# A causal attention stage without TensorE transposes: turns by VectorE and DMA, x loaded a batch sooner, work between the pairs spread evenly

## The chip, the core and the metric

The kernel runs on one NeuronCore of one Trainium2 chip. The core has a matrix engine (TensorE, PE in the profile; its weight loads are PEld), VectorE (DVE), ScalarE (ACT), GpSimd (POOL) and SyncE (SP), whose queue issues almost all DMAs here. Each engine works through its own list in order; semaphores tie the lists together. Matmuls write to PSUM, which has eight banks of 128 x 512 float32. The metric is device time in microseconds (us) from one launch to its end; less is better.

## What is computed

Two attention models run one after the other on the same `x`. The change touches the first, causal attention with a layer norm ahead and a residual; the second (two layers of windowed attention with a gated feed-forward part) is left as it is.

```python
x = x + _L0_attn_ref(_layernorm(x, axis=-1), wq, bq, wk, bk, wv, bv, wo, bo)
x = x + _L0_ffn_ref(_layernorm(x, axis=-1), ...)

def _L0_attn_ref(x, wq, bq, wk, bk, wv, bv, wo, bo):      # x: 4 batches, 1024 tokens, 256 wide
    q = proj(wq, bq); k = proj(wk, bk); v = proj(wv, bv)  # 16 heads of 16
    scores = jnp.einsum('bhqd,bhkd->bhqk', q, k) * scale
    mask = jnp.triu(jnp.full((t, t), NEG, jnp.float32), k=1)
    attn = jax.nn.softmax(scores + mask, axis=-1)
    out = jnp.einsum('bhqk,bhkd->bhqd', attn, v)
    return out.transpose(0, 2, 1, 3).reshape(b, t, d) @ wo + bo
```

Everything is float32.

## The kernel before

**Tiling.** A *chunk* n is four heads of one batch: 4 batches x 4 = 16 chunks, b, c = divmod(n, 4). Its four heads lie in four 32-row strips of two buffers `qbuf` and `kbuf` (head j in rows 32j to 32j+15; row 32j+16 of `kbuf` is a constant). So four small matmuls, one per strip, run in TensorE side by side. Each score is computed twice: first as `s`, queries on partitions, from which VectorE takes each query's maximum (line 375 with the mask on the diagonal, line 380 elsewhere), then as `t`, keys on partitions and the maximum already subtracted, of which ScalarE takes the exponential into `et` (line 388). GpSimd zeroes the masked part of the diagonal blocks (line 394). The product of `et` with `v_sb` accumulates in `av`; a column of ones in `v_sb` gives the softmax's denominator in row 16 of each strip.

**Order.** The list of each engine is written out by hand (`manual_schedule`). A chunk has twelve *units*. In unit u, `pair(n, u, 0)` issues two `t` of chunk n and two `s` of chunk n+1, `products(n, u-2)` follows, then `pair(n, u, 1)` with the other two heads, then the unit's *fillers*. Units have 512, 384, 256, 128, five times 512, 384, 256 and 128 columns. Before chunk 0 there is a round n = -1 with maxima alone; chunk 15 has no `s`.

**Fillers** are set out by `fillers(n)`:
- `norm`, `prep_x`, `prep_a`, `prep_b`, in the second chunk of a batch, for the next batch: statistics and `xn` on VectorE, the transpose `pxn` on TensorE, its copy to `xnT` on ScalarE, then `v`, with the bias added by VectorE;
- `project`: a quarter of q or k (`pp`), copied with its bias to `dense` by ScalarE; `spread`: eight DMAs on SP from `dense` to the strips of `qbuf` and `kbuf`;
- `put_maxima`: four transposes `pm` of the maxima, which VectorE subtracts from `qbuf` into `qTm` (line 413), the operand of `t`;
- `put_out`: four transposes `po` of the copied `av`, then division by the denominator into `y_sb`;
- `out_a`, `out_b`, `out_c`: transposes `pot`, output projection `pr`, residual and next layer norm; after the last one of a batch x goes to DRAM (`x_keep`) and, where there is one, x of batch b+2 is loaded.

**PSUM.** `t` has three banks (`pat`), `s` three (`pas`), and `av` and all fillers share two (`pa1`).

The second stage turns its operands with VectorE transposes of 32 x 32 blocks into `turned` (lines 783 to 806), from which sixteen DMAs (line 814) carry the blocks to their places in `ring_sb`. It starts with the matmuls `pq`, `pk`, `pv` of line 715.

Of the kernel before, what the change touches and what calls it, by code (L numbers as in the profile page):

```python
# [49 lines left out]
def kernel_body(  # L50
# [26 lines left out]

    la = ctx.enter_context(tc.tile_pool(name="la", bufs=1))
    actx = ExitStack()
    xpool = actx.enter_context(tc.tile_pool(name="xpool", bufs=2))  # L80
# [86 lines left out]

    with actx:
# [3 lines left out]
        a3 = actx.enter_context(tc.tile_pool(name="a3", bufs=3))  # L172
# [3 lines left out]
        pas = actx.enter_context(tc.tile_pool(name="pas", bufs=3, space=PSUM))  # L176
        pa1 = actx.enter_context(tc.tile_pool(name="pa1", bufs=2, space=PSUM))

        def one(name):
            return pa1.tile([P, 512], F32, tag="one", name=name)  # L180
# [23 lines left out]
        qbuf = [aw.tile([P, T], F32, name=f"qbuf{i}") for i in range(3)]  # L204
        kbuf = [aw.tile([P, T], F32, name=f"kbuf{i}") for i in range(4)]

        nmax = []
        for i in range(NW):
            m = aw.tile([P, 4, STRIP], F32, name=f"nmax{i}")
            nmax.append(m)  # L210

        def clear():

            nc.gpsimd.memset(qbuf[1], 0.0)
            nc.gpsimd.memset(kbuf[1], 1.0)
            for v in v_sb:
                nc.gpsimd.memset(v[:, :, H * VW :], 0.0)
                nc.gpsimd.memset(
                    v[:, :, 0 : H * VW].rearrange("p k (h s) -> p k h s", s=VW)[
                        :, :, :, ONE : ONE + 1  # L220
                    ],
                    1.0,
                )
            nc.gpsimd.memset(qbuf[2], 0.0)
            for i in (2, 3):
                nc.gpsimd.memset(kbuf[i], 1.0)
# [10 lines left out]
        stats, xnTs, qTms, dense, avs_, mxs = {}, {}, {}, {}, {}, {}  # L237
        qTs, kTs = (lambda n: qbuf[n % 3]), (lambda n: kbuf[n % 4])

        def norm(b, t0=0, t1=NW):  # L240

            if t0 == 0:
                xnTs[b] = a1.tile([P, 2, T], F32, tag="xnT", name=f"xnT_{b}")
# [9 lines left out]
        def prep_x(b, t2):  # L253

            for t in (2 * t2, 2 * t2 + 1):
                xn = a3.tile([P, D], F32, tag="xn", name=f"xn_{b}_{t}")
                mean, rs = stats.pop((b, "t", t))
                nc.vector.tensor_scalar(xn, xs[b][:, t, :], mean, rs, ALU.subtract, ALU.mult)
                stats[b, "xn", t] = xn

        def prep_a(b, t2):

            pt = one(f"pxn_{b}_{t2}")
            for i in range(2):
                xn = stats.pop((b, "xn", 2 * t2 + i))
                for c in range(2):
                    o = c * 256 + i * P
                    nc.tensor.transpose(pt[:, o : o + P], xn[:, c * P : (c + 1) * P], ident)
            nc.scalar.copy(
                xnTs[b][:, :, t2 * 256 : (t2 + 1) * 256], pt.rearrange("p (c n) -> p c n", c=2)  # L270
            )

        def prep_b(b, t2):

            pv = one(f"pv_{b}_{t2}")
            for i in range(2):
                t = 2 * t2 + i
                for c in range(2):
                    nc.tensor.matmul(  # L279
                        pv[:, i * D : (i + 1) * D], lhsT=xnTs[b][:, c, t * P : (t + 1) * P],  # L280
                        rhs=wv_sb[:, c, :], start=(c == 0), stop=(c == 1),
                    )
            for i in range(2):
                nc.vector.tensor_tensor(
# [4 lines left out]
                    rows_c[:, 0, :].rearrange("p (h d) -> p h d", h=H),  # L289
                    ALU.add,  # L290
# [4 lines left out]
            )  # L295

        def project(b, d, which, h):
# [8 lines left out]
            for k in range(2):  # L306
                nc.tensor.matmul(  # L307
                    pp[:, 0:256], lhsT=wt[:, k, d * P : (d + 1) * P], rhs=xnTs[b][:, k, ts],
                    start=(k == 0), stop=(k == 1),
# [18 lines left out]
        def pair(n, u, pr):  # L328
# [15 lines left out]
            if th:  # L344
# [3 lines left out]
                for j, h in enumerate(th):  # L348
                    r = slice(32 * h, 32 * h + 32)
                    todo.append((j, 0, ts[h][:, c0:512], kTs(n)[r, kt * P : (kt + 1) * P],  # L350
                                 qTms[n][r, qb * 512 + c0 : (qb + 1) * 512]))
            if sh:
# [6 lines left out]
                for j, h in enumerate(sh):  # L359
                    r = slice(32 * h, 32 * h + 32)  # L360
# [4 lines left out]
            if sh:  # L365
                if i >= 4 and piece == 0 and pr == 0:
                    mxs[n + 1, i] = a5.tile([P, 4, 2], F32, tag="mx", name=f"mx_{n + 1}_{i}")
                for h in sh:
                    if i >= 4:
                        acc = mxs[n + 1, i][:, h, piece : piece + 1]  # L370
                    else:
                        acc = nmax[i][:, h, ONE : ONE + 1]
                    if diag:
# [3 lines left out]
                            scale=1.0, scalar=-3.0e38, op0=ALU.add, op1=ALU.max, accum_out=acc,  # L377
# [3 lines left out]
                if piece and (pr or first):  # L381
                    nc.vector.tensor_reduce(
                        nmax[i][:, :, ONE], mxs.pop((n + 1, i)), AX.X, ALU.max
                    )
# [17 lines left out]
        def put_maxima(n, qb):  # L402

            if qb == 0:
                qTms[n] = a2.tile([P, T], F32, tag="qTm", name=f"qTm_{n}")
            pm = one(f"pm_{n}_{qb}")
            for i in range(4):
                nc.tensor.transpose(
                    pm[:, i * P : (i + 1) * P],
                    nmax[4 * qb + i].rearrange("p j s -> p (j s)"), ident,  # L410
                )
            qs = slice(qb * 512, (qb + 1) * 512)
            nc.vector.tensor_tensor(qTms[n][:, qs], qTs(n)[:, qs], pm, ALU.subtract)

        def products(n, u):
# [3 lines left out]
            if kt == 0:  # L419
                avs_[n, "acc"] = one(f"av_{n}_{qb}")  # L420
            av = avs_[n, "acc"]
            ets, c0 = avs_.pop((n, u))
            for j in range(4):
                nc.tensor.matmul(  # L424
                    av[32 * j : 32 * j + 32, c0:512],
                    lhsT=v_sb[b % 2][:, kt, VW * (4 * c + j) : VW * (4 * c + j) + STRIP],
                    rhs=ets[j // 2][:, j % 2, c0:512],
                    start=(kt == 0), stop=(kt == 4 * qb + 3),
                )
            if kt == 4 * qb + 3:  # L430
                avs = a2.tile([P, 512], F32, tag="avs", name=f"avs_{n}_{qb}")
# [3 lines left out]
        def put_out(n, qb):  # L435

            b, c = divmod(n, NC4)
            avs = avs_.pop((n, "out", qb))
            po = one(f"po_{n}_{qb}")
            for i in range(4):  # L440
# [833 lines left out]
```

## Time and profile before

| what | value (us where no unit is given) |
|---|---|
| median of 3 runs (lowest, highest) | 1977.33 (1976.79, 1978.14) |
| profiled execution, its own time | 1976.66 |
| its span | 1974.9 |
| first pair of chunk 0 | 54.2 |
| first pair of chunk 15 | 716.7 |
| first matmul of the second stage (`pq`) | 760.0 |
| chunks 4, 5, 6, 7 (a whole batch) | 45.8, 46.7, 42.4, 44.8 |
| chunk 13 (no next batch to prepare) | 39.5 |
| causal stage, share of SP's DMAs in 54 to 717 us | 9% of the DMA engines |
| granted TensorE clock, whole span | 0.988 of full speed |

The chunk times are the distances between the first pairs of successive chunks on TensorE's timeline. In the stretch from 54 to 717 us VectorE is busy for 476.6 of 663 us, ScalarE for 365.5 and GpSimd for 135.6.

How the profile is read: in a list of groups each line has the source line, the engine, the operation, what it writes and reads, its shape and count, then the busy time in us and the mean of one in ns, then the engine's idle time just ahead and what ended it. A float32 matmul shows as two instructions (two passes). In a timeline the columns are the start, the duration, the engine, the line and operation; in brackets the idle time before it and what ended it.

### The profile page before, as it was taken

The page shows a single profiled execution, that of the slowest core. Times are in us where ns is not written, and L with a number is a line of the kernel's source. Part 1 is how long each engine was busy: PE and PEld are TensorE (multiplying, and loading weights), DVE is VectorE, ACT ScalarE, POOL GpSimd, SP SyncE. Part 2 cuts the span into 40 slices and gives each one's busy share as a digit, 9 for nine tenths or more (in the row PEclk, how much of TensorE's full clock was granted, in tenths as well). Part 3 has the DMA queues.
Part 4 walks back from the last instruction along what each step waited for, and adds up shares of the span by engine and source line. Part 5 has one row for each costly group of instructions (what it writes and reads, how often), then busy time and mean ns, then how long its engine had stood idle before and what let it go on. Part 6 is the DMA issues. An engine that isn't in the chain of part 4 may idle for free.

```text
span 1974.9 us, 46934 instructions
## 1 busy us (share of the span) xinstructions
PE 1921.1 (97%) x17356; PEld 1091.1 (55%) x17356; DVE 1364.2 (69%) x4196; ACT 1000.8 (51%) x2627; POOL 932.4 (47%) x1177
## 2 busy tenths in 40 slices
PE   8999999999999997989899999999999999999999
PEld 5444444444444434646565666666666666566575
DVE  6686777677667745676776776776777687677633
ACT  1556555555555563545455555555545544555521
POOL 3122122112211115775765765765675676676521
PEclk8999999999999999999899999999999999999999
DMA  3021010101001001045555555565566565665520
GB/s 96 19 72 23 12 54 3 26 28 33 15 20 33 1 1 68 10 83 91 101 87 95 97 106 90 107 125 102 92 145 113 99 115 106 108 113 99 102 49 22
DMA packets 763347, 136.26 MB, mean 69 GB/s; under 512 B 733952, under 2 KB 756208, under 8 KB 762608
## 3 DMA queue, kind: packets, MB, share of 16 engines
q1 hardware_dynamic: 762864, 133.00, 34.6%
q8 instruction: 138, 2.26, 0.5%
q14 instruction: 89, 0.73, 0.1%
q10 hardware_dynamic: 256, 0.26, 0.1%
HBM read 20.99 MB, written 8.39 MB: 15 GB/s over the span
## 4 chain that ended last, share of the span: by engine, by line
PE 86%; DVE 5%; SPq 3%; issue 1%; POOL 1%; DMA 1%; ACT 1%; DVEq 0%; ACTq 0%; POOLq 0%
PE t L364 15%; PE pag L1074 14%; PE av L424 7%; PE pf L1098 7%; PE pw L984 5%; PE pq L715 5%; PE pk L715 5%; PE plo L942 4%; PE pv L715 4%; PE ls L862 3%; PE pp L307 3%; SPq L814 3%; PE s L364 3%; PE pr L472 1%; PE pv L279 1%
## 5 line engine op out<-in xcount | busy, mean ns | idle before, releaser
L388 ACT ACTIVATE et<-t 128x512 f32<-128x512 f32 (+2 forms) x744 | 327.6, 492 | 278.1 <-PE s L364 248.5
L364 PE MATMUL s<-kbuf,qbuf 32*128 32x512 f32 (+3 forms) x1440 | 381.7, 532 | 2.2 <-DVE nmax L375 1.5
L364 PE MATMUL t<-qTm,kbuf 32*128 32x512 f32 (+2 forms) x1488 | 371.2, 532 | 0.8 <-ACT et L388 0.2
L394 POOL TENSOR_SCALAR_AFFINE_SELECT et<-et 128x256 f32<-128x256 f32 x256 | 103.8, 407 | 462.0 <-ACT et L388 461.8
L1074 PE MATMUL pag<-hnT,w 128*128 128x512 f32 x704 | 312.0, 593 | 0.8 <-DVE hnT L1058 0.8
L375 DVE CUSTOM_DVE_ANT_0 junk<-s,mask_c 128x512 f32<-128x512 f32 (+1 forms) x480 | 216.4, 488 | 89.6 <-PE s L364 85.8
L895 ACT ACTIVATE e<-e,lnmx 128x192 f32<-128x192 f32 (+2 forms) x512 | 224.1, 439 | 47.4 <-DVE lnmx L888 46.9
L364 PEld LDWEIGHTS t<-qTm,kbuf 32*128 32x128 f32 x1488 | 135.5, 183 | 169.4 <-ACT et L388 127.7
L909 POOL TENSOR_SCALAR e<-e,lrsum 128x192 f32<-128x192 f32 (+2 forms) x512 | 205.7, 423 | 19.5 <-DVE lrsum L906 13.9
L1074 PEld LDWEIGHTS pag<-hnT,w 128*128 128x128 f32 x704 | 131.7, 190 | 142.5 <-issue 134.2
L380 DVE TENSOR_REDUCE mx<-s 128x1 f32<-128x512 f32 x240 | 154.7, 686 | 68.1 <-PE s L364 66.3
L754 POOL TENSOR_TENSOR rn<-ss,mhalf 128x16 f32<-128x16 f32 x64 | 188.1, 2939 | 5.3
L1098 PE MATMUL pf<-w,act 128*128 128x256 f32 x768 | 173.1, 379 | 0.0
L751 POOL TENSOR_TENSOR rot<-rot,m 128x1024 f32<-128x1024 f32 x64 | 151.1, 2362 | 38.6 <-DVE m L732 34.9
L424 PE MATMUL av<-et,v_sb 128*32 128x512 f32 (+3 forms) x1536 | 163.5, 498 | 0.6 <-POOL et L394 0.6
L1098 PEld LDWEIGHTS pf<-w,act 128*128 128x128 f32 x768 | 146.1, 190 | 26.4 <-issue 7.2
L1088 DVE SCALAR_TENSOR_TENSOR act<-pag,cols_sb,ge 128x512 f32<-128x512 f32 x80 | 59.3, 741 | 141.6 <-ACT ge L1087 102.9
L364 PEld LDWEIGHTS s<-kbuf,qbuf 32*128 32x128 f32 x1440 | 140.4, 183 | 17.5 <-DVE nmax L375 6.0
L888 DVE CUSTOM_DVE_ANT_0 e<-ls,mask_h 128x192 f32<-128x192 f32 x408 | 116.8, 350 | 22.2 <-PE ls L862 22.1
L984 PE MATMUL pw<-wlo,loT 128*128 128x256 f32 x512 | 127.5, 393 | 0.7 <-ACT loT L975 0.7
L715 PE MATMUL pq<-wqkv,hT 128*128 128x512 f32 x256 | 122.6, 602 | 3.8 <-ACT hT L697 3.8
L756 POOL TENSOR_TENSOR rot<-rot,rn 128x1024 f32<-128x1024 f32 x64 | 121.7, 1901 | 5.0
(287 smaller groups left out, 3214.3 us busy)
## 6 DMA issues: line engine op xcount, KB each, us to landing
ring_sb<-turned SPq DMA_DIRECT2D x896, 96.0 KB
qbuf<-dense SPq DMA_DIRECT2D x128, 32.0 KB
x_keep<-x SPq DMA_DIRECT2D x4, 1024.0 KB
xr<-x_keep SPq DMA_DIRECT2D x8, 512.0 KB
out_dram<-y_sb SPq DMA_DIRECT2D x16, 256.0 KB
kbuf<-dense SPq DMA_DIRECT2D x120, 32.0 KB
x<-in_x_dram SPq DMA_DIRECT2D x3, 1024.0 KB
wqkv<-in_wqkv_dram SPq DMA_DIRECT2D x2, 1536.0 KB
```

Of the source, the lines that this page charges most:

```text
L364: nc.tensor.matmul(o, lhsT=lhsT, rhs=rhs, start=True, stop=True)
L375: nc.vector.tensor_tensor_reduce(out=junk[:, 0:w], in0=ss[h][:, 0:w], in1=mask_c[:, 512 - w : 512], scale=1.0, scalar=-3.0e38, op0=ALU.add ...
L380: nc.vector.tensor_reduce(acc, ss[h][:, 0:w], AX.X, ALU.max)
L388: nc.scalar.activation(et[:, h % 2, c0:512], ts[h][:, c0:512], AF.Exp, scale=ASCALE)
L424: nc.tensor.matmul(av[32 * j : 32 * j + 32, c0:512], lhsT=v_sb[b % 2][:, kt, VW * (4 * c + j) : VW * (4 * c + j) + STRIP], rhs=ets[j // 2] ...
L715: nc.tensor.matmul(pq[i], lhsT=lhs[c], rhs=wt[:, c, i * INNER : (i + 1) * INNER], start=(c == 0), stop=(c == 1),)
L754: nc.gpsimd.tensor_tensor(rn[:, :, 0], ss, mhalf, ALU.pow)
L895: nc.scalar.activation(e[:, i, lo:nk], e[:, i, lo:nk], AF.Exp, bias=nmx[:, h : h + 1], scale=-1.0, accum_out=sums[:, h : h + 1],)
L909: nc.gpsimd.tensor_scalar(e[:, i, lo:nk], e[:, i, lo:nk], rsum[:, h : h + 1], 1.0, ALU.mult, ALU.mult)
L984: nc.tensor.matmul(pw[:, 0:D], lhsT=oT[:, c, :], rhs=wt[:, c, :], start=(c == 0), stop=(c == 3))
L1074: nc.tensor.matmul(pg[half], lhsT=wt[:, c, ff * P : (ff + 1) * P], rhs=hnT[:, c, :], start=(c == 0), stop=(c == 1),)
L1098: nc.tensor.matmul(pf[:, 0:D], lhsT=act[:, f, i * P : (i + 1) * P], rhs=wt[:, f, :], start=(f == 0), stop=(f == NF - 1),)
```

## The change

- Maxima: VectorE writes them into one tile `nmax`, in 16 columns for each half of the queries; `put_maxima` transposes it on VectorE (`mt`), writes it by four DMAs to a DRAM tile `way`, and reads it back by one into row 16 of each strip of `qbuf`. Row 16 of `kbuf` is -1, so `t` itself subtracts the maximum; `qTm` is gone. `s` uses only the 16 rows of q and k.
- Output: `put_out` transposes `avs` on VectorE (32 x 32 blocks), GpSimd divides, `put_oT` transposes back and four DMAs carry the strips to `oT`, the operand of `out_b`. `out_a` is gone.
- Input: for batches 1 to 3 `xn` is made by GpSimd, turned by VectorE into `xturn` and carried to `xnT` by sixteen DMAs for each half of a batch (`turn_x`). It starts in the first chunk of a batch and goes on in the second.
- The bias of v goes through `wo` once (`bias`) into the row that is added to x.
- `project`, `prep_b` and `out_b` issue each matmul as four of 32 columns (`strips`).
- ScalarE copies `v` and the output projection; GpSimd adds the residual and makes `y_sb`.
- In units without a matmul filler, `products` is issued in two halves, one after each pair.
- `s` and the fillers share four banks, `av` has one, `t` keeps three. `qbuf` has four buffers, x three; x of batch 2 is loaded in chunk 1, x of batch 3 after batch 0 is done.
- Memsets at the start: three of q and k go to VectorE ahead of the first norm, three of later buffers to GpSimd in the round n = -1.

```diff
-    xpool = actx.enter_context(tc.tile_pool(name="xpool", bufs=2))
+    xpool = actx.enter_context(tc.tile_pool(name="xpool", bufs=3))
...
-        pas = actx.enter_context(tc.tile_pool(name="pas", bufs=3, space=PSUM))
-        pa1 = actx.enter_context(tc.tile_pool(name="pa1", bufs=2, space=PSUM))
+        pas = actx.enter_context(tc.tile_pool(name="pas", bufs=4, space=PSUM))
+        pa1 = actx.enter_context(tc.tile_pool(name="pa1", bufs=1, space=PSUM))
         def one(name):
-            return pa1.tile([P, 512], F32, tag="one", name=name)
+            return pas.tile([P, 512], F32, tag="s", name=name)
...
+        xturn = aw.tile([P, GRP, 2, 4, 32], F32, name="xturn")
+        oT = aw.tile([P, 2, T], F32, name="oT")
         def clear():
-            nc.gpsimd.memset(qbuf[1], 0.0)
-            nc.gpsimd.memset(kbuf[1], 1.0)
+            nc.vector.memset(qbuf[1], 0.0)
+            nc.vector.memset(kbuf[1], -1.0)
+            nc.vector.memset(qbuf[2], 0.0)
...
+        def clear_more():
+            nc.gpsimd.memset(kbuf[2], -1.0)
+            nc.gpsimd.memset(qbuf[3], 0.0)
+            nc.gpsimd.memset(kbuf[3], -1.0)
...
+        def strips(o, lhsT, rhs, k):
+            for r in range(0, P, STRIP):
+                nc.tensor.matmul(
+                    o[r : r + STRIP], lhsT=lhsT[:, r : r + STRIP], rhs=rhs,
+                    start=(k == 0), stop=(k == 1), skip_group_check=True,
+                )
...
+        def turn_x(b, g, i):
+            for t in (2 * i, 2 * i + 1):
+                nc.vector.transpose(
+                    xturn[:, t].rearrange("p c j r -> p (c j r)"), stats.pop((b, "xn", GRP * g + t))
+                )
+            if i == 0:
+                return
+            dst = xnTs[b][:, GRP * g : GRP * g + GRP].rearrange("p t c n -> p (t c) n")
+            src = xturn.rearrange("p t c j r -> p (t c) j r")
+            for d in range(4):
+                for a in range(4):
+                    j = (a + d) % 4
+                    nc.sync.dma_start(
+                        dst[32 * j : 32 * j + 32, :, 32 * a : 32 * a + 32],
+                        src[32 * a : 32 * a + 32, :, j, :],
+                    )
...
         def put_maxima(n, qb):
-            pm = one(f"pm_{n}_{qb}")
-            for i in range(4):
-                nc.tensor.transpose(
-                    pm[:, i * P : (i + 1) * P],
-                    nmax[4 * qb + i].rearrange("p j s -> p (j s)"), ident,
-                )
-            qs = slice(qb * 512, (qb + 1) * 512)
-            nc.vector.tensor_tensor(qTms[n][:, qs], qTs(n)[:, qs], pm, ALU.subtract)
+            mt = a2.tile([P, STRIP], F32, tag="mt", name=f"mt_{n}_{qb}")
+            nc.vector.transpose(mt, nmax[:, qb, :])
+            way = keep4.tile([4 * GRP, P], F32, tag="way", name=f"way_{n}_{qb}")
+            for a in range(4):
+                nc.sync.dma_start(
+                    way[:, 32 * a : 32 * a + 32], mt[32 * a : 32 * a + 4 * GRP, :]
+                )
+            nc.sync.dma_start(
+                qTs(n)[ONE:P:STRIP, qb * 512 : (qb + 1) * 512],
+                way.rearrange("(j i) x -> j (i x)", j=4),
+            )
...
         def put_out(n, qb):
+            t1 = a1.tile([P, 16, 32], F32, tag="t1", name=f"t1_{n}_{qb}")
+            nc.vector.transpose(t1.rearrange("p q s -> p (q s)"), avs_.pop((n, "out", qb)))
+            rec = a2.tile([P, 16, 1], F32, tag="rec", name=f"rec_{n}_{qb}")
+            nc.vector.reciprocal(rec, t1[:, :, ONE : ONE + 1])
+            nc.gpsimd.tensor_tensor(
+                t1[:, :, 0:HD], t1[:, :, 0:HD], rec.to_broadcast([P, 16, HD]), ALU.mult
+            )
+            avs_[n, "t1", qb] = t1
+        def put_oT(n, qb):
             b, c = divmod(n, NC4)
+            t3 = a1.tile([P, 512], F32, tag="t3", name=f"t3_{n}_{qb}")
+            nc.vector.transpose(t3, avs_.pop((n, "t1", qb)).rearrange("p q s -> p (q s)"))
+            for j in range(4):
+                r = (c % 2) * 64 + j * HD
+                nc.sync.dma_start(
+                    oT[r : r + HD, c // 2, qb * 512 : (qb + 1) * 512],
+                    t3[STRIP * j : STRIP * j + HD, :],
+                )
...
+            if c == 0:
+                if b:
+                    quarters(n, b, 1, 3, 0, 2, 4, 6, 8)
+                    outs(n, 7, b - 1, 2)
+                    outs(n, NU, b - 1, 3)
...
+                put(n, 9, spread, n + 2, 1)
+                put(n, NU, spread, n + 3, 1)
+            if c == 0 and more:
+                for i, u in enumerate((5, 7, 9, 10)):
+                    put(n, u, norm, b + 1, 2 * i, 2 * i + 2)
+                put(n, 8, prep_x, b + 1, 0)
+                put(n, 10, turn_x, b + 1, 0, 0)
+                put(n, 10, prep_x, b + 1, 1)
+                n += 1
+                put(n, 0, turn_x, b + 1, 0, 1)
+                put(n, 1, prep_x, b + 1, 2)
+                put(n, 2, prep_x, b + 1, 3)
+                put(n, 3, turn_x, b + 1, 1, 0)
+                put(n, 4, turn_x, b + 1, 1, 1)
+                quarters(n, b + 1, 0, 0, 5, 6, 8, 10)
+                n += 1
+                quarters(n, b + 1, 0, 4, 0, 2, 3, 4)
...
                 for u in range(NU):
                     pair(n, u, 0)
                     m, w = (n, u - LAG) if u >= LAG else (n - 1, u - LAG + NU)
+                    apart = 0 <= n < NCH - 1 and not any(fn in on_pe for fn, _ in f[u])
+                    apart = apart and UNITS_T[w][1] > 0
                     if m >= 0:
-                        products(m, w)
-                    if n % NC4 == 1 and u == 8:
-                        put_maxima(n + 1, 0)
+                        products(m, w, 0 if apart else None)
                     pair(n, u, 1)
+                    if m >= 0 and apart:
+                        products(m, w, 1)
                     for fn, a in f[u]:
                         fn(*a)
```

A slot NU in `put` is unit 0 of the next chunk. In the new lists SP has, from unit 11 of a batch's first chunk on: the five DMAs of `put_maxima(n + 1, 1)`, in chunk 1 the loads of `wqkv`, the tables and `wlo`, the eight DMAs of `spread(n + 3, 1)`, the sixteen of `turn_x(., 0, 1)`, in chunk 5 and 9 the store `x_keep` (in 5 the load of x too), the four of `put_oT(n - 1, 1)`, and the sixteen of `turn_x(., 1, 1)`.

## The prediction

> **What bounds the kernel now.** I read the busy rows first, then the groups of the first 800 us by form, then TensorE's timeline block by block. The change lies in the causal stage, which ends with the first matmul `pq` at 760.0 us.
>
> ```profile
> PE 1921.1 (97%) x17356; PEld 1091.1 (55%) x17356; DVE 1364.2 (69%) x4196; ACT 1000.8 (51%) x2627; POOL 932.4 (47%) x1177
> L364 PEld LDWEIGHTS t<-qTm,kbuf 32*128 32x128 f32 x1488 | 135.5, 183 | 169.4 <-ACT et L388 127.7
> ```
>
> TensorE is busy for 97% of the span, so one would think that every removed matmul pays. But the weight loads of `t` stood 127.7 us behind `et`: the next `t` waits until ScalarE has emptied a bank. The timeline shows one such wait:
>
> ```profile
> 342.64 0.59 PE L364 MATMUL s<-kbuf,qbuf 32*128 32x512 f32 x1
> ...
> 343.16 0.43 PE L424 MATMUL av<-et,v_sb 128*32 128x128 f32 x8
> 343.29 1.29 DVE L380 TENSOR_REDUCE mx<-s 128x1 f32<-128x512 f32 x2 [1.13 <-PE s L364]
> 343.31 1.08 ACT L388 ACTIVATE et<-t 128x512 f32<-128x512 f32 x2 [0.64 <-PE s L364]
> 343.51 0.69 PE L364 MATMUL t<-qTm,kbuf 32*128 32x512 f32 x1
> 343.52 0.69 PE L364 MATMUL s<-kbuf,qbuf 32*128 32x512 f32 x1
> 343.95 0.69 PE L364 MATMUL t<-qTm,kbuf 32*128 32x512 f32 x1
> 344.04 0.69 PE L364 MATMUL s<-kbuf,qbuf 32*128 32x512 f32 x1
> ```
>
> The second `t` starts 0.44 us after the first, when the first exponential has ended; the second `s` 0.09 later, when the first maximum has freed the third `s` bank.
>
> From start to start, a block of TensorE takes for 512/384/256/128 columns: a pair 1.07/0.86/0.64/0.43, products 1.00/0.78/0.57/0.36, a projection 1.06, `pv` or `pr` 1.925, four transposes 0.585. These values repeat to 0.01. A pair is longer only when too little lies ahead of it: 1.36 after a block of 0.57, 1.57 after 0.36, 2.04 right after a pair (which then takes 0.96), 1.07 after 1.00 or more. In each case the pair ahead, the block between and the excess make **1.93 us** (1.07+0.57+0.29; 1.07+0.36+0.50): a floor under the step from pair to pair (1.60, 1.25, 0.97 for the other widths). Chunks 0 to 14 (54.2 to 716.7) take 662.5 us: blocks 602.8, plus 49.9 for the floor, plus 9.8 unexplained.
>
> **The change, part by part.**
>
> *Transposes.* `pm`, `po`, `pot` and three batches of `pxn` go: 32+32+16+12 = 92 blocks of 0.585, 54 us of TensorE. But most stood between pairs that the floor keeps apart: a unit of 512 columns with a transpose takes 4.00 us (1.07+1.00+1.07+0.585+0.27), and one without filler takes 4.00 too (2.04+1.00+0.96, chunk 13).
>
> *Products in halves.* Where a unit has no filler, half a product block stands ahead of each pair: two floors, 3.86, each half costing a further 0.15 (the products' time beyond their columns).
>
> *Four `s` banks.* The second `s` no longer waits for VectorE; what is left is ScalarE. The 0.09 of the timeline makes the floor 1.85 (I take 1.53, 1.18, 0.92).
>
> *Strips.* A projection in four 32-column strips costs what products with 2x512 columns cost, as those too are four strips with 128 rows: 1.00, `pv` and `pr` 1.85. Bounds: that, and 0.4 more each if the sixteen loads show.
>
> Adding the new order of blocks by these prices: blocks 557.9, floors 57.9, **615.8 us** for chunks 0 to 14, against 652.7 before by the same sum. So 54 us of transposes are worth 37.
>
> *VectorE, ScalarE, GpSimd.* Out go `qTm` 32x0.683, `y_sb` from `po` 13.6, the `v` addition 13.4, `nmax` 10.5, and `x`, `xn`, `y_sb` of 14, 24 and 30 instructions, 90 us in all; in come 64 transposes of 128x512 at 0.67 and 24 of 128x256 at 0.40 (the rows of `turned`), with the small `mt` some 58 us. A chunk has about 29 us of maxima on VectorE, so the first chunk of a batch, which now has the whole norm (four times 1.35: two `st` of 0.41, two `mv` of 0.18, one `ve` of 0.17), gets 41 us against TensorE's 40. Units 9 to 11 there give it 9.7 us (maxima 6.2, two norms, a turn of 0.8) for TensorE's 7.2: it ends 2.8 us behind, and the next pair waits about 1.3. Three times: +4. ScalarE gains 4 us and GpSimd 65, both far from full.
>
> *The turn through SP.* A batch's `xn` is turned by VectorE into `xturn`, one buffer for four tiles, and sixteen DMAs carry it to `xnT`. `turn_x(.,1,0)`, unit 3 of a batch's second chunk, writes `xturn` again, so VectorE, in order, waits there until all sixteen have read it. The second stage has this very scheme, and its wait:
>
> ```profile
> 866.45 2.03 SPq L814 DMA_DIRECT2D ring_sb<-turned  x3
> ...
> 870.34 1.25 DVE L783 STREAM_TRANSPOSE turned<-rot 128x1024 f32<-128x1024 f32 x1 [4.76 <-DMA ring_sb<-turned]
> ```
>
> VectorE goes on 1.9 us after the last issue ended. Issues of the same shape (8x32) stand 0.65 apart. SP's queue from the chunk's start: the maxima `mt` at +3.0 (VectorE's lag); four `way` DMAs 2.4, their landing 2.0, the read 0.6 (+8.0); spread of chunk n+3, 8x0.63 (+13.0); sixteen turns, 10.4 (+23.4); VectorE free at +25.3. It reached the wait near +14.5. Behind it stand t3 of the last chunk, the four maxima of unit 4 and then the turn of tiles 6 and 7. TensorE fills its four `s` banks in unit 4 and is out at 12.4 (units 0 to 3 by the prices above) + 1.3 + 3.7 (unit 4) = +17.4; a bank is free at 25.3+0.8+0.65+0.1 = 26.9. **9.5 us** idle.
>
> The Trainium skill speaks against such DMAs: "DMA: Bandwidth & Descriptors", Anatomy of one DMA, puts about 2.0 us of fixed cost on each (for GpSimd's path). Sixteen in a row would be 32 us, an estimate; the rows show them overlapped, 10.4+1.9, and I take the rows.
>
> An idle TensorE also loses its clock. By the rows:
>
> ```profile
> 760.03 3.79 PE L715 MATMUL pq<-wqkv,hT 128*128 128x512 f32 x4 [3.09 <-ACT hT L697]
> 763.61 3.14 PE L715 MATMUL pk<-wqkv,hT 128*128 128x512 f32 x4
> 766.59 1.88 PE L715 MATMUL pv<-wqkv,hT 128*128 128x512 f32 x4
> ```
>
> The same four matmuls take 3.79, 3.14, then 1.88 after 3.09 us idle: 3.2 lost. The skill ("TensorE: Matmul & The Clock Gate", Part 1) says that an idle window of some 3.4 us halves the clock until a busy one has passed, which would lose 1.7, an estimate. I take 3.0. So 12.5 for the batches at chunks 5 and 9. In chunk 1 the loads of `wqkv`, tables and `wlo` come into SP's queue just before the spread; in this trace those 3.1 MB fill the DMA engines for 11 us (103 to 114), where the spread's reuse of semaphores makes SP wait for them: +7.5, and TensorE comes 1.1 earlier (no `out_b` in unit 0): 21. Together **46**, less 2 of floors that lie in it. Bounds: 20 (SP ahead by half) and 60.
>
> *Other moves on queues.* The maxima of the upper half pass SP with five DMAs, 7 us, ahead of a use four units (13 us) on: hidden, unless SP is behind; after the turns it is, but that chunk's end is then later too. In chunk 5 SP also waits 3.5 us (its wait for `x_keep<-x` here: 7.0 in 2) before the load of x for batch 3; that falls behind the first turn and delays the second, whose columns are first used in the next chunk: hidden by some 10 us. Otherwise the earlier load of x brings nothing: no row of before waits for x after the start.
>
> *Start.* Here
>
> ```profile
> 14.07 6.84 DVE L258 TENSOR_SCALAR xn<-x,mv,rs_a 128x256 f32<-128x256 f32 x4 [1.13 <-POOL rs_a L158]
> ```
>
> four `xn` take 6.84 us beside GpSimd's memsets (13.98 to 19.5), 0.41 each elsewhere. Those memsets move: three to VectorE at its idle start, three later. That gives 5 us, of which ScalarE's DMA issues (to 18.0) keep half. The first chunk of maxima, bound by VectorE, loses 2 us of work. Together -4; between -6 and 0, if VectorE's three memsets meet GpSimd's (1.7 each, as here).
>
> *End.* Chunk 15 loses 3 us of transposes; after it the chain `avs`, two VectorE transposes, four DMAs takes 7.9 us where 4.75 were, at a colder clock: +1 net, between -2 and +4.
>
> **Sum.** 615.8 + 4 + 46 - 2 + 5 (half of the unexplained 9.8, as four banks absorb some) = 668.8 for chunks 0 to 14: +6.3. With -4 and +1: +3.3. The profiled run took 1976.66 (span 1974.9), so 1980.0; the median of the runs is 0.67 above it: **1981 us**, no change within 0.2% (4 us, which is about what a measurement here can tell).
>
> **Rivals.**
> 1. *The turn is mostly hidden.* The same, with SP ahead: VectorE's lag doesn't hold `way`, loads overlap the spread. The wait is 20 instead of 46: 1955. For it: SP is mostly free in this stage; its longest waits there are for `dense` (318.5 us in 23). Against: the 4.76 wait above. From 38 on it isn't faster. Chance 0.27.
> 2. *The floor stays.* ScalarE alone sets 1.93, and four banks and halves buy nothing: floors 72.7 instead of 57.9, +15: 1996. For it: the stall is the same for diagonal maxima, which VectorE takes 0.08 longer for. It decides as soon as the floor is over 1.87. Chance 0.23.
> 3. *Strips don't overlap* in sequence: 0.35 more on each block, +28: 2008. Against: the products' 1.00. Chance 0.05.
>
> The forecast (1970 to 1990) has 0.45. Range 1953 to 2003, which leaves out the lower third of rival 1 and the third. Faster by over 4 us (under 1973.4): rival 1 and 0.05 of the middle, 0.32. Within: 0.20 of the middle. Slower (over 1981.3): the middle's other 0.20, rivals 2 and 3: 0.48.
>
> **What would show it.** Right: no transposes but four `pxn` on TensorE before 760 us; VectorE waits of about 10, 10 and 18 us for `xnT<-xturn` in chunks 1, 5, 9, TensorE's clock low after each; 512-unit without filler about 3.7. Wrong: waits under 5 us; units of 3.3 (no floor) or 4.0; `pp` blocks of more than 1.1; the second stage changed by more than 2 us.

## The result, and the profile after

| | before | changed |
|---|---|---|
| median of 8 runs (lowest, highest) | 1977.74 (1971.23, 1983.43) | 1986.57 (1981.74, 1991.55) |
| ratio, 95% interval | | 1.0037 [1.0020, 1.0053] |
| profiled execution, its own time / its span | 1976.66 / 1974.9 | 1991.55 / 1989.8 |
| first pair of chunk 0 | 54.2 | 59.1 |
| chunks 0 to 14 | 662.5 | 663.8 |
| chunks 1, 5, 9 | 46.7, 46.7, 46.7 | 65.2, 52.9, 57.1 |
| chunks 2, 3, 4, 13, 14 | 42.4, 44.8, 45.8, 39.5, 39.0 | 42.3, 42.9, 40.6, 37.0, 35.4 |
| first pair of chunk 15 to the first `pq` | 43.3 | 43.7 |
| first `pq` to the last matmul | 1211.3 | 1219.6 |

All times in us. The change made the kernel slower by 0.4%. The profiled execution of the changed kernel was the slowest of its eight, so the difference of the two profiles, 14.9 us, is 6 us above that of the medians.

The page of the changed kernel: busy time by engine, the granted clock in 40 slices of 50 us, and the weight loads of `t` that the prediction started from.

```profile
PE 1899.3 (95%) x19234; PEld 1033.1 (52%) x19234; DVE 1350.0 (68%) x4092; ACT 1005.3 (51%) x2646; POOL 1029.5 (52%) x1268
...
PEclk7959998998899998989999999999999999999999
...
L415 PEld LDWEIGHTS t<-qbuf,kbuf 32*128 32x128 f32 x1488 | 145.4, 190 | 171.4 <-ACT et L439 114.8
```

TensorE's busy time fell by 22 us and the time rose. The wait of these loads for `et` fell only from 127.7 to 114.8 us. The row of the clock is the new thing: a 5 in the third slice, where before no slice was under 8. Of the twelve chunks other than 1, 5 and 9, nine are 1.6 to 6.3 us shorter, and 2, 6 and 10 are as long as before. Chunks 1, 5 and 9 took that back, and they are those in which most of `turn_x` works.

The wait that was forecast is there. VectorE's timeline in chunk 1, then SP's:

```profile
116.37 0.08 DVE L427 DVE_READ_ACCUMULATOR2_ANT nmax<- 128x1 f32 x1
130.68 0.77 DVE L295 STREAM_TRANSPOSE xturn<-xn 128x256 f32<-128x256 f32 x2 [14.23 <-DMA xnT<-xturn]
131.38 0.67 DVE L507 STREAM_TRANSPOSE t<-t 128x512 f32<-128x512 f32 x1
```

```profile
118.09 0.51 SPq L374 DMA_DIRECT2D kbuf<-dense  x1
118.70 10.47 SPq L305 DMA_DIRECT2D xnT<-xturn  x16
```

VectorE stands 14.2 us until the sixteen DMAs have read `xturn`. They are issued in 10.5 us, and the last read ends 1.5 us after. In chunk 5 the wait is 8.2 us, in chunk 9 6.8. TensorE runs out of `s` banks behind it and stands for 8.5, 6.0 and 4.6 us; in chunk 1:

```profile
132.68 1.21 PE L415 MATMUL s<-kbuf,qbuf 16*128 16x512 f32 x1 [8.52 <-DVE mx L433]
```

The half clock wasn't expected in that measure. Busy time in windows of 10 us (PE, PEld, DVE, ACT, POOL, each with its count), then the granted clock, the DMA engines' share and GB/s:

```profile
20.00:30.00 10.00, 6.75 (x66) 3.20 (x58) 4.53 (x16) 1.79 (x4) 0.00 (x0) 0.82 0.20 44
30.00:40.00 10.00, 9.57 (x54) 4.82 (x58) 7.93 (x26) 0.00 (x0) 4.93 (x4) 0.50 0.39 108
40.00:50.00 10.00, 10.00 (x64) 3.48 (x56) 4.87 (x8) 0.65 (x2) 0.00 (x0) 0.50 0.12 38
...
110.00:120.00 10.00, 9.90 (x68) 4.25 (x72) 3.16 (x18) 3.17 (x10) 6.53 (x9) 0.50 0.69 204
...
140.00:150.00 10.00, 10.00 (x58) 2.28 (x58) 3.90 (x7) 3.50 (x8) 0.62 (x1) 0.54 0.22 35
```

Two of the same windows in the kernel before:

```profile
30.00:40.00 10.00, 10.00 (x40) 6.15 (x41) 9.04 (x31) 0.00 (x0) 0.00 (x0) 0.61 0.30 66
140.00:150.00 10.00, 10.00 (x84) 5.00 (x84) 6.77 (x30) 4.49 (x13) 3.52 (x7) 1.00 0.00 0
```

In the changed kernel TensorE is busy all the time from 40 to 50 us and from 140 to 150, and the clock is half for all or nearly all of it. The rule that the prediction weighed, that a busy window brings the clock back, does not fit this. Nor did the wait start the half clock of chunk 1: by the clock's records it lasts from 101.4 to 149.2 us, so it begins 15 us before VectorE stands and some 23 us before TensorE does.

### The profile page after: what moved, and what is told of

The parts are those of the page before. It is cut to its first block, busy times and chain, and to the rows that moved or that the text cites. A ratio compares the mean times of both kernels' runs of the same rounds, so it can differ in the third digit from the quotient of the medians.

```text
span 1989.8 us, 51315 instructions
## 1 busy us (share of the span) xinstructions
PE 1899.3 (95%) x19234; PEld 1033.1 (52%) x19234; DVE 1350.0 (68%) x4092; ACT 1005.3 (51%) x2646; POOL 1029.5 (52%) x1268
## 4 chain that ended last, share of the span: by engine, by line
PE 85%; SPq 5%; DVE 4%; issue 2%; DMA 2%; POOL 1%; ACT 1%; ACTq 0%; DVEq 0%; POOLq 0%
PE t L415 15%; PE pag L1144 14%; PE pf L1168 8%; PE av L478 7%; PE pw L1054 6%; PE pq L785 5%; PE pk L785 5%; PE pv L785 5%; PE plo L1012 4%; PE ls L932 4%; SPq L884 3%; PE pp L252 3%; PE pv L252 2%; PE s L415 2%; PE pr L252 1%
## 5 line engine op out<-in xcount | busy, mean ns | idle before, releaser
L415 PE MATMUL s<-kbuf,qbuf 16*128 16x512 f32 (+3 forms) x1440 | 387.8, 561 | 19.5 <-DVE mx L433 19.1
L415 PE MATMUL t<-qbuf,kbuf 32*128 32x512 f32 (+2 forms) x1488 | 402.5, 559 | 2.5 <-ACT et L439 2.4
L415 PEld LDWEIGHTS t<-qbuf,kbuf 32*128 32x128 f32 x1488 | 145.4, 190 | 171.4 <-ACT et L439 114.8
L979 POOL TENSOR_SCALAR e<-e,lrsum 128x192 f32<-128x192 f32 (+2 forms) x512 | 205.7, 423 | 20.4 <-DVE lrsum L976 14.9
L478 PE MATMUL av<-et,v_sb 128*32 128x256 f32 (+5 forms) x2240 | 187.9, 408 | 4.3 <-POOL et L445 2.8
L1168 PEld LDWEIGHTS pf<-w,act 128*128 128x128 f32 x768 | 145.8, 190 | 26.6 <-issue 7.2
L415 PEld LDWEIGHTS s<-kbuf,qbuf 16*128 16x128 f32 x1440 | 143.6, 191 | 29.7 <-DVE mx L433 23.5
L427 DVE CUSTOM_DVE_ANT_0 junk<-s,mask_c 128x512 f32<-128x512 f32 (+3 forms) x240 | 106.9, 485 | 61.6 <-PE s L415 59.1
L427 DVE CUSTOM_DVE_ANT_0 junk<-s,mask_c,mx 128x512 f32<-128x512 f32 (+3 forms) x240 | 121.0, 546 | 37.6 <-PE s L415 36.4
L958 DVE CUSTOM_DVE_ANT_0 e<-ls,mask_h 128x192 f32<-128x192 f32 x408 | 116.9, 350 | 23.2 <-PE ls L932 23.2
L478 PEld LDWEIGHTS av<-et,v_sb 128*32 128x32 f32 x2240 | 45.3, 109 | 163.6 <-issue 119.0
```

What stands on the lines that cost most here:

```text
L415: nc.tensor.matmul(o, lhsT=lhsT, rhs=rhs, start=True, stop=True)
L427: nc.vector.tensor_tensor_reduce(out=junk[:, 0:w], in0=ss[h][:, 0:w], in1=mask_c[:, 512 - w : 512], scale=1.0, scalar=mxs[n + 1, i][:, h : ...
L478: nc.tensor.matmul(av[32 * j : 32 * j + 32, lo:hi], lhsT=v_sb[b % 2][:, kt, VW * (4 * c + j) : VW * (4 * c + j) + STRIP], rhs=ets[j // 2][ ...
L979: nc.gpsimd.tensor_scalar(e[:, i, lo:nk], e[:, i, lo:nk], rsum[:, h : h + 1], 1.0, ALU.mult, ALU.mult)
L1168: nc.tensor.matmul(pf[:, 0:D], lhsT=act[:, f, i * P : (i + 1) * P], rhs=wt[:, f, :], start=(f == 0), stop=(f == NF - 1),)
```

## The experiments

Three theories were put against each other.

1. *The turn.* The loss is the wait for `xturn`: what lies ahead of the sixteen DMAs in SP's queue sets it.
2. *The array's work.* The clock comes back only when enough of the array works in a window, and `s` with 16 rows instead of 32 does half the work in the same time.
3. *Code.* TensorE's additional matmuls shift where its code is loaded, and the second stage stalls there.

Under the second theory one number can be worked out from the trace for each window of 3.41 us (all low stretches, but for the one that the end of a run cuts off, are multiples of it): the sum over the matmuls of rows x columns of the array in use, times the columns streamed, as a share of what a 128 x 128 array does when it streams 512 columns in 0.43 us (`pq`: four such passes in 1.71 us). It is called the **share** below.

### Two buffers for the turn

```diff
-        xturn = aw.tile([P, GRP, 2, 4, 32], F32, name="xturn")
+        xturns = [aw.tile([P, GRP, 2, 4, 32], F32, name=f"xturn{g}") for g in range(2)]
...
         def turn_x(b, g, i):
+            xturn = xturns[g]
```

> Two xturn buffers, one for each half of a batch, so that VectorE's turn of tiles 4 and 5 no longer waits for the first sixteen DMAs. Theory 1 (the wait for xturn is the loss): chunks 1, 5 and 9, now 65.2, 52.9 and 57.1 us, come to about 40 each, the 14.2, 8.2 and 6.8 us of VectorE waiting go, and the time falls by 45 to 55 us to 1930 to 1942. If in addition the clock stays low for as long as the array does little (theory 2), chunk 1 stays at half clock for some 20 us from its start, as a low window lies ahead of the wait, and it takes 47 rather than 40. Rival (SP's queue is the bound, and the wait only turns up at the next use, of xnT or of mt): less than 15 us gained.

Measured: 1974.78, ratio to before 0.9978 [0.9966, 0.9989], some 12 us less than the changed kernel. Expected were 45 to 55. In the profile, which is of its slowest execution, chunks 1, 5 and 9 took 58.0, 51.7 and 57.3: the first gained 7.2 us, the others 1.2 and nothing. VectorE no longer waits for `xturn`. TensorE does, at the first projection of the new batch in unit 5 (its timeline):

```profile
127.38 1.06 PE L416 MATMUL s<-kbuf,qbuf 16*128 16x512 f32 x1
131.84 1.51 PE L252 MATMUL pp<-xnT,wq_sb 128*32 128x256 f32 x12 [3.41 <-DMA xnT<-xturn]
```

The rival was right: the same sixteen DMAs have a second waiter, the reader of `xnT`, and the gain stayed under its 15 us. The clock stayed low from 102 for 41.0 us in chunk 1, and for 27.3 us in chunk 9.

### The turn ahead of the spread

```diff
-                put(n, NU, spread, n + 3, 1)
+                put(n, NU + 2, spread, n + 3, 1)
```

> spread(n+3, 1), eight DMAs, is issued two units later, behind the first sixteen turn DMAs instead of ahead of them; one xturn buffer as in the changed kernel. Theory 1 (VectorE waits for the last turn DMA, and what lies ahead in SP's queue sets that): the wait of chunk 1 falls from 14.2 to about 4 us, those of chunks 5 and 9 from 8.2 and 6.8 to about 3 and 2, the total by 18 to 28 us to 1959 to 1969. Rival (the DMAs' own transfer, not the queue, or the loads of 3.1 MB in chunk 1, set it): less than 8 us gained.

Measured: 1973.81, ratio 0.9975 [0.9965, 0.9984], some 12 us less than the changed kernel. VectorE's waits fell from 14.2, 8.2 and 6.8 to 8.2, 4.4 and 2.7, chunks 1, 5 and 9 to 55.6, 49.7 and 50.1. So the order in SP's queue sets the wait, as theory 1 says, but in chunk 1 only by 6 instead of 10 us: the sixteen issues, which now stand right behind the 3.1 MB of loads, took 15.1 instead of 10.5 us, 1.8 of them in waits for loads `wlo` and `tab`. The gain of the time was two thirds of the lower end expected.

### s over 32 rows

```diff
-                    r = slice(32 * h, 32 * h + HD)
+                    r = slice(32 * h, 32 * h + STRIP)
```

> s reads 32 rows of each strip again instead of 16; all else as in the changed kernel. Row 16 then takes part: it holds an older chunk's maximum times -1, a shift of all scores of a query, which the softmax takes out again. Theory 2 (the clock comes back only when a 3.4 us window has enough rows x columns of the array at work, about 0.38 of the whole, and pairs at half clock with 16 rows give 0.29 to 0.38 where 32 rows would give 0.37 to 0.45): the low stretch at the start shrinks from 23.9 to about 10 us, those after the waits in chunks 1 and 9 end some 10 us sooner each; first pair of chunk 0 at about 52 instead of 59.1, total 12 to 17 us less, 1970 to 1975. Rival (the clock looks at idle time alone): no change, 1984 to 1989, low stretches of 24, 48 and 20 us as before.

Measured: 1982.53, ratio 1.0021 [1.0013, 1.0029], some 3 us less than the changed kernel, a quarter of what was expected. The low stretches did what theory 2 says: 10.2 us instead of 23.9 at the start, 23.9 instead of 47.8 in chunk 1, 13.7 instead of 20.5 in chunk 9; first pair of chunk 0 at 54.3. The same windows as above:

```profile
30.00:40.00 10.00, 9.57 (x66) 4.96 (x65) 7.60 (x26) 0.00 (x0) 4.93 (x4) 0.61 0.33 81
40.00:50.00 10.00, 9.49 (x116) 4.05 (x112) 8.46 (x18) 1.94 (x6) 0.00 (x0) 1.00 0.20 68
...
140.00:150.00 10.00, 10.00 (x100) 3.13 (x96) 8.40 (x20) 6.39 (x13) 1.78 (x4) 1.00 0.35 103
```

The time gained less than the clock, because the wait for the turn ends when SP is done and TensorE is only sooner at it: it stood 17.4, 7.8 and 8.1 us in chunks 1, 5 and 9, where it stood 8.5, 6.0 and 4.6. Chunks 1 and 9 gained 3.4 and 3.2 us in this profile, the start 4.8.

### The kernel before, with s over 16 rows

The same line of the kernel before, the other way round: `32 * h + 32` becomes `32 * h + HD` for `s`.

> The kernel before, with s cut to the 16 rows of q and k, as in the changed kernel; nothing else. Theory 2 (array work in a window decides when the clock comes back): the two low stretches at the start, 6.8 and 10.2 us, grow to 20 us or more together with s alone at work there, first pair of chunk 0 at 57 to 60 instead of 54.2; chunks 0 to 14 as before, as nothing makes TensorE idle there. Total 2 to 5 us more. Rival (idle time alone): no change, low stretches 6.8 and 10.2.

Measured: 1989.28, ratio 1.0054 [1.0037, 1.0071], 10.7 us more, twice the most expected. First pair of chunk 0 at 57.0, with a stretch of 17.1 us instead of 10.2. The expectation was wrong in that nothing would happen in the chunks: chunks 1, 5 and 9 took 48.2 instead of 46.7, chunk 4 49.0 instead of 45.8. Its windows, the kernel before first:

```profile
255.00:260.00 5.00, 5.00 (x35) 2.33 (x35) 3.87 (x7) 2.75 (x5) 0.00 (x0) 1.00 0.00 0
260.00:265.00 5.00, 5.00 (x30) 1.78 (x29) 4.24 (x10) 2.17 (x4) 0.70 (x1) 1.00 0.51 210
```

```profile
255.00:260.00 5.00, 5.00 (x30) 2.07 (x28) 4.48 (x11) 2.56 (x5) 0.69 (x1) 0.92 0.00 0
260.00:265.00 5.00, 5.00 (x22) 1.24 (x24) 1.90 (x4) 1.67 (x3) 0.00 (x0) 0.50 0.00 0
```

Nobody waits here. TensorE is busy for all of the ten us in both, and in the second the clock falls to half: the window from 255.8 us has a share of 0.37. The rows alone cost half a per cent, with no wait on a turn in the program.

### The bias of v ahead of ScalarE's issues

```diff
-            nc.scalar.copy(bv[:, 0:D], pb[:, 0:D])
-            po = one("pbias_o")
+            nc.scalar.copy(bv[:, 0:D], pb[:, 0:D])
+            stats["bv"] = bv
+
+        def bias():
+            bv = stats.pop("bv")
+            po = one("pbias_o")
...
-        plan[n][0] += [(spread, (0, 1, nc.scalar)), (spread, (1, 0)), (spread, (1, 1))]
+        plan[n][0] += [(bias_a, ()), (spread, (0, 1, nc.scalar)), (spread, (1, 0)), (spread, (1, 1))]
```

The lines ahead of `def bias` become `bias_a`; `bv` gets a tile of its own.

> The bias of v is transposed and copied at the end of unit 0's projections, ahead of ScalarE's four DMA issues, and only its product with wo stays in unit 1, so TensorE doesn't stand 3.25 us. Theory A (this stall and the half clock that follows put the start back): first pair of chunk 0 at 51 to 55 instead of 59.1, total 4 to 8 us less. Rival B (round -1 is bound by VectorE's maxima and falls to half clock with or without the stall): under 2.5 us gained, first pair at 57 or later.

Measured: first pair of chunk 0 at 51.7, 7.4 us sooner, as theory A says; low stretches at the start of 6.8 and 3.4 us. The time was 1984.07, ratio 1.0027 [1.0014, 1.0040]: 2 us less, which the intervals don't separate from nothing. In this profile chunks 5 and 9 differ from the changed kernel's by +3.8 and -3.7 us though no edit is there: a low stretch begins where the windows of 3.41 us happen to lie. That is what the runs of these kernels scatter by. The stall itself, on the changed kernel's timeline:

```profile
23.83 3.57 ACTq L374 DMA_DIRECT2D kbuf<-dense  x4
...
24.23 0.44 PE L335 MATMUL pbias<-ident,rows_c 128*128 128x128 f32 x2
...
27.50 0.37 ACT L339 COPY bv<-pbias 128x256 f32<-128x256 f32 x1 [3.70 <-DMA kbuf<-dense]
...
27.92 2.08 PE L342 MATMUL pbias_o<-wo_sb,bv 128*128 128x256 f32 x4 [3.25 <-ACT bv L339]
```

ScalarE issues four DMAs for 3.6 us, the copy of `bv` stands behind them, and TensorE behind the copy.

### Halves and banks, one at a time

`apart = False` for the first, `bufs=3` for the pool of `s` for the second. Each has one execution, of 1993.14 and 2019.03 us, and is read by its chunks alone.

> Products are never issued in halves; all else as in the changed kernel. It asks which part brought units without filler from 4.00 us before to about 3.2. If the halves did it: chunks 13 and 14, now 37.0 and 35.4, go to 39 to 40, units without filler to 3.8 to 4.0. If the fourth bank of s did it: both stay within 0.7 us.

> Three banks for s and the fillers instead of four (one bank of PSUM is left unused); all else as in the changed kernel. If the fourth bank took the stall away: chunks 13 and 14 go from 37.0 and 35.4 to 38.5 to 40, and the chunks with projections by 1 to 2 us, as each projection now takes one of three. If the halves alone did it: both stay within 0.7 us.

Without halves chunks 13 and 14 took 39.2 and 38.0 instead of 37.0 and 35.4, so the halves bring 2.2 to 2.6 us in such a chunk. A unit of 512 columns without filler took 3.92 us, where it took 3.99 in the kernel before: the fourth bank alone brings 0.07. With three banks and halves chunk 14 took 36.9 instead of 35.4, so the bank is worth 1.5 us once the pairs stand evenly. (Chunk 13 took 43.9; a low stretch of 13.7 us lies in it.) Where a projection takes one of the banks it is worth more: chunks 4 and 8 took 45.0 instead of 40.6. Neither was the whole of it.

### No strips

`strips` issues one matmul of 128 columns instead of four.

> project, prep_b and out_b issue one matmul of 128 columns again instead of four of 32; all else as in the changed kernel. In the causal stage a pp block should take 1.06 instead of 1.00 and pv and pr 1.92 instead of 1.85, up to 6 us more by chunk 15, less where it lies under another wait (the single-strip rival of the prediction would have it 28 us shorter). Theory 3 (TensorE's 1878 additional matmuls shift where its code is loaded, and the four new stalls of 1.4 to 2.5 us on ls near 850, 1180, 1490 and 1815 us come from that): the distance from the first pq to the end falls from 1219.6 to about 1212, and loads of code from 153 to about 138. Rival (the second stage is longer for another reason, its start or the clock): 1218 or more.

Measured: 1989.95, ratio 1.0060 [1.0040, 1.0080], not separable from the changed kernel. The twelve chunks without a turn took 2.3 us more together. Theory 3 fell as it was put: the loads of code (the DMA queue `instruction` of the page) went from 153 to 141, and the second stage still took 1219.7. What the changed kernel's trace shows is two stalls like this one, the other of 2.5 us at 1819.5, in which TensorE waits for nothing that is recorded:

```profile
1492.66 0.52 PE L932 MATMUL ls<-ring_sb 64*64 64x64 f32 x21 [2.10 <-issue]
```

The kernel before and that with 16 rows, whose lists on TensorE are equally long, have neither, and take 1211.3 and 1211.7 from the first `pq` to the end. Without halves, with a list of another length, it took 1213.2. What sets these stalls is left open.

### Together

The changed kernel with two buffers, `s` over 32 rows, the bias ahead of the issues, `spread(n + 3, 1)` in `NU + 3`, the loads for the second stage in chunk 2, and `quarters(n, b + 1, 0, 0, 7, 8, 9, 10)` for the first four projections. The second differs from it by the line of `s` alone, the third by 34 matmuls behind the last `put_oT`.

> The changed kernel with two xturn buffers, s over 32 rows, the bias of v copied ahead of ScalarE's DMA issues, spread(n+3, 1) three units later, the loads for the second stage in chunk 2 instead of 1, and the first four projections of a new batch in units 7 to 10 instead of 5, 6, 8, 10. Theories 1 and 2 together: first pair of chunk 0 at 50 to 53, chunks 1, 5 and 9 at 40 to 43 us instead of 65.2, 52.9 and 57.1, no low stretch over 4 us between 60 and 740 us; total 50 to 65 us below the changed kernel, 1922 to 1937. Rival (SP's queue and the sixteen turn DMAs are still too late for the projections or for mt, the maxima): a chunk of 46 or more, total above 1945.

> The same with s over 16 rows, so that the rows alone differ. Theory 2: 6 to 12 us more than with 32 rows, with low stretches at the start and in the first units of chunks that follow a batch's first one. Rival (rows matter only where TensorE had stood idle for a window, which no longer happens): under 2 us more.

> The first of these, with 34 matmuls of 128 columns into an unused bank behind the last put_oT, where TensorE waits 8.4 us for the output's way through VectorE and four DMAs. Theory 2: the last projection takes 3.7 instead of 5.3 us and the low stretches of 10.2 us at the end of the stage go; the gain is 2 to 5 us. Rival (the chain through VectorE and the DMAs is the bound at the start of the second stage too): under 1 us.

Measured: **1943.69**, ratio to before 0.9818 [0.9802, 0.9835]; with 16 rows **1965.39**, 0.9921 [0.9899, 0.9943]; with the 34 matmuls 1942.93, 0.9807 [0.9789, 0.9824].

The first is 1.8% faster than the kernel before and 43 us faster than the changed one, though 7 us short of what was expected. First pair of chunk 0 at 48.3; chunks 1, 5 and 9 took 42.4, 48.5 and 46.4, the last two where the rival put them. TensorE has no idle time over 1 us in chunk 5 any more. Left there are a low stretch of 10.2 us (6.8 in chunk 9), which was to be gone, and VectorE's lag from the chunk ahead: unit 0 takes 6.1 us, where it takes 3.9 in chunk 6.

Rows alone make 21.7 us of difference, nearly twice the most that theory 2 expected. Chunk 1, with 32 rows and then with 16:

```profile
90.00:100.00 10.00, 9.44 (x116) 4.26 (x112) 7.95 (x34) 5.70 (x15) 7.50 (x13) 1.00 0.17 29
100.00:110.00 10.00, 10.00 (x96) 3.75 (x90) 8.55 (x22) 6.13 (x13) 2.95 (x5) 1.00 0.26 47
110.00:120.00 10.00, 10.00 (x95) 3.04 (x88) 7.94 (x16) 6.14 (x12) 1.23 (x3) 1.00 0.26 49
```

```profile
90.00:100.00 10.00, 9.88 (x80) 3.74 (x72) 7.60 (x32) 3.60 (x9) 5.10 (x9) 0.69 0.04 6
100.00:110.00 10.00, 9.90 (x74) 4.25 (x72) 5.22 (x25) 3.56 (x11) 6.82 (x9) 0.50 0.28 45
110.00:120.00 10.00, 10.00 (x68) 3.27 (x64) 6.04 (x12) 4.13 (x8) 0.49 (x2) 0.50 0.26 53
```

TensorE is equally busy in both, and issues in the second 222 matmul instructions in the time of 307. The low stretch lasts 30.7 us, nine windows; the first eight have shares of 0.25 to 0.35, and the ninth, with a projection in it, 0.39. With 32 rows the dip at the chunk's start has a share of 0.38 and the clock stays.

The filled gap: the last projection took 3.2 instead of 6.0 us and chunk 15 41.7 instead of 44.4, as theory 2 says. The time is not separable from the version without it: in its profile chunk 2, where nothing was changed, took 2.5 us more, with a low stretch of 3.4 us in it. Not tried: which of the other parts of this version could be left out, and the turn's DMAs on another engine's queue.

## Why the prediction came out as it did

It gave 1981 in a range of 1953 to 2003 and 0.48 for slower; measured are 1986.57 and a ratio just clear of one. Its steps against the changed kernel's profile:

- *Blocks, floors and leftovers of the twelve chunks without a turn* (all of 0 to 14 but 1, 5, 9). The prices give 496.1 for them, and with their part of the 5 us put down as unexplained 500. Measured: 488.7. The projections took 1.00 as priced. The blocks make 449.9 of it, which leaves 38.8 where 46.2 of floors were added. The floor of 1.85 was too high: units 6 to 8 of chunk 14 took 3.59 on the mean, not 3.70. Rivals 2 and 3 are refuted: the floor did not stay, and strips overlap.
- *The turn.* The mechanism was right, and its place: VectorE waits in chunks 1, 5 and 9, and in chunk 1 SP waits 4.6 us in the spread for the loads ahead of it, as put. These chunks took 175.2 where the prices without a turn give 119.7, so the turn, with VectorE's lag, cost 55.5. The sum had 46, less 2, plus 4 for the lag. With `s` over 32 rows they took 168.3, which is 48.6 over the prices, the sum to 0.6 us, and TensorE stood 17.4, 7.8 and 8.1 us, where 18 and twice 9.5 were put. So the 7 us beyond the sum go with the rows of `s`, as far as single profiles tell: with the bias moved, chunks 5 and 9 differed by some 4 us each way without an edit there. The clock's mechanism was wrong: "An idle TensorE also loses its clock" and "I take 3.0" put the half clock behind the wait, where in chunk 1 it began some 23 us ahead of TensorE's wait and lasted 47.8 us.
- *The start.* "Together -4" measured +4.9. This step failed. The memsets brought their 5 us: unit 1 of round -1 comes at 23.2, where it came at 28.2. What was left out is `bias`, whose copy stands behind ScalarE's DMA issues, and that round -1 has `s` almost alone on TensorE, at 16 rows. With the bias ahead of the issues the start is 2.5 us sooner than before, more than half of what the step was to bring; with 32 rows instead it is as late as before (54.3).
- *The end.* +1 was forecast, +0.4 measured to the first `pq`. The chain behind the last product is longer, as put:

```profile
759.43 5.27 PE L252 MATMUL pr<-wo_sb,oT 128*32 128x256 f32 x56 [8.46 <-DMA oT<-t]
...
766.60 1.98 PE L785 MATMUL pq<-wqkv,hT 128*128 128x512 f32 x4 [0.58 <-ACT hT L767]
```

- *The second stage* was taken as unchanged and is 8.3 us longer in this profile. The prediction had named a change of more than 2 us there as a sign of being wrong, and the sign came. 2.4 us come in its first 40 us (2.4 to 3.2 in every variant of the changed kernel). It starts warm now: `pq` and `pk` take 1.98 and 1.88 us, where they took 3.79 and 3.14. But GpSimd now makes `y_sb`, two in 2.4 us; ScalarE's copy of `edge` stands for it, and the copies for VectorE's rotations stand behind that copy:

```profile
771.40 0.19 ACT L773 COPY edge<-hT 128x1 f32<-128x1 f32 x1 [4.77 <-POOL y_sb L548]
771.50 0.59 ACT L794 ACTIVATE m<-pq 128x512 f32<-128x512 f32 x1
```

So `rot` reaches TensorE only 0.5 us sooner after the first `pq` than before. The rest of the 3 us gained goes into a longer wait, and the half clock behind it, from 784.1 to 790.9, costs another 2.9. The kernel before, then the changed one:

```profile
776.59 1.09 PE L825 MATMUL pt<-ident,rot 128*128 128x128 f32 x8 [1.75 <-POOL rot L756]
...
779.65 1.98 PE L715 MATMUL pq<-wqkv,hT 128*128 128x512 f32 x4
```

```profile
782.63 1.09 PE L895 MATMUL pt<-ident,rot 128*128 128x128 f32 x8 [3.83 <-POOL rot L826]
...
786.56 3.78 PE L785 MATMUL pq<-wqkv,hT 128*128 128x512 f32 x4
```

The prediction counted the move of `y_sb` to GpSimd as free. The other 6 us come in steps at stalls that the kernel before does not have, 1.4 us at 849.9 for `ring_sb<-turned`, and the two of 2.1 and 2.5 named above; their cause stays open.

In all: +1.3 for chunks 0 to 14 (forecast +6.3), +4.9 (-4), +0.4 (+1), +8.3 (0). That the time lay in the range was luck in part: floors and leftovers some 12 us too high hid half of the 25 us that the turn, the start and the second stage cost beyond the sum. One cause that the prediction did not look at runs through the first two of these: it counted `s` with 16 rows as equal to `s` with 32, because its duration is equal. In the changed kernel as it stands the rows are worth only some 3 us, as the waits stand beside them; with the waits mostly gone they are worth 21.7.

## What to carry to other kernels

Check for each stretch what share of the array TensorE's matmuls use, not only that it is busy: cutting unused rows out of `s` saved no time here, and halved the clock of everything around it. When a wait on a buffer is taken away with a second buffer, look for the next reader of the same transfers; here the buffer alone brought 12 us of the 45 to 55 expected, and with the queue ordered and the reader moved later as well the wait went; which of these it needs was not tried. A cheap operation that hands a value from one engine to another must not stand behind DMA issues on the engine between them.

## What the runs showed of the hardware

Over the 13 profiles of this case there are 7522 windows of 3.41 us. Of 7006 with a share of 0.39 or more none was followed by half clock, whatever the clock in it. Of 430 with a share under 0.36, all but 8 were followed by half clock. Between lie 86 windows that went either way. Some windows:

| kernel, window from (us) | TensorE busy | share | clock in it, then after it |
|---|---|---|---|
| changed, 43.4: `s` alone | 1.00 | 0.13 | half, half |
| changed, 142.4 | 1.00 | 0.38 | half, half |
| changed, 145.8 | 1.00 | 0.40 | half, full |
| changed, `s` over 32 rows, 133.4 | 1.00 | 0.45 | half, full |
| before, 104.0 | 0.93 | 0.48 | full, full |
| before, `s` over 16 rows, 105.6 | 0.93 | 0.33 | full, half |
| all together with 16 rows, 107.5 | 1.00 | 0.32 | half, half |

The clock is real: in chunk 1 of the changed kernel a matmul of 512 columns takes 1.06 instead of 0.59 us in the low stretches.

Neither busy time, nor columns streamed alone, nor rows counted in full strips of 32 separates the windows so. Of the 299 windows at half clock in which TensorE is over 90% busy, a share of 0.38 puts 8 on the wrong side; the best threshold in full strips puts 38 there, and in columns streamed 101: windows with 1.8 times the array's columns streamed (four strips side by side) stayed low. At half clock a window holds about half as many matmuls. In the version with all together and 16 rows, windows at full clock between 145 and 185 us have a share of 0.66 on the mean, and those of the low stretch 0.25 to 0.35, so it stays down until something wider comes. That is how one dip of a window became a low stretch of 30 us.

The Trainium skill, "TensorE: Matmul & The Clock Gate", Part 1, has the window's length (3413 ns) and the two clocks, and these traces agree with both: the low stretches are multiples of 3.41, and the clock is 0.50 or 1.00. It says that one busy window brings the clock back. Here windows that were 97% to 100% busy did not, eight in a row; the measurement decides. The share is worked out from the traces, and no run varied it at a fixed program other than through the rows of `s`.
